# Routing the second mixture of experts inside the attention ahead of it, in pieces, with result adds, next blocks and zone loads ordered behind named instructions

## The chip, the core and the metric

The kernel runs on one core of a Trainium2 chip. A core has five engines, each with an instruction queue that it works off in order: TensorE (PE, matmuls and transposes; its weight loads are listed as PEld), VectorE (DVE), ScalarE (ACT), GpSimd (POOL) and SyncE (SP), which here only reads registers and issues DMAs. ACT and POOL issue some DMAs as well. An instruction waits for its operands, and all that stands behind it in its queue waits too. The metric is the device time of one execution in microseconds (us), lower is better; a profile adds what each engine did when.

## The reference, cut to what matters

A residual stream of 16 sequences of 256 tokens, 4096 tokens of 128 numbers in float32, passes six layers, each with a layer norm ahead of it:

```
x = x + 0.5 * moe(ln(x))      # 8 experts, the best 2 of each token, plus a gated shared expert
x = x + gqa(ln(x))            # softmax attention: 16 query heads on 4 key heads, 8 numbers a head
x = x + 0.5 * moe(ln(x))      # the same weights again
x = x + 0.5 * zones(ln(x))    # the best 3 of 8 feed-forwards, chosen once for a whole sequence
x = x + mla(ln(x))            # attention with latent keys and values, 8 heads
x = x + 0.5 * zones(ln(x))
```
```
def moe(x):
    scores = softmax(x @ gate_w.T)                 # 8 experts
    w = scores * in_top2(scores)
    g, u = split(x @ experts_gate_up)              # 2 x 176, of each expert
    out = sum_e(w[e] * ((silu(g) * u) @ experts_down[e]))
    shared = (silu(x @ sg.T) * (x @ su.T)) @ sd.T  # 352 wide
    return out + sigmoid(x @ shared_gate.T) * shared
```

The change touches the way into and out of both mixtures of experts (MoE), and what is interleaved with the first attention. It computes the same.

## The kernel before

**Tiling.** The stream stays on chip in eight tiles `xs[t]`, one for each block of 512 tokens (two sequences). Two blocks are a pair (four pairs, `q`), two pairs are a part (two parts). The layers follow one another, so the stages in time are: first MoE, attention (`gqa`), second MoE, zones, `mla`, zones.

**The MoE.** A pair is routed in four steps. `norm_pair` normalises its eight 128-token groups (`normalised`, L272: per group `bn_stats` and `bn_aggr`, then one reciprocal square root of some ten small DVE instructions, then eight applies, alternately on DVE and ACT). `turn_pair` transposes the rows on PE (L401). `choose` multiplies them with the router (L417) and finds the best two experts in some 20 small DVE instructions (L425 to L446). `place_pair` counts with three matmuls (L467 to L473) where each token's row goes in a buffer in memory that has a region for each expert, and POOL writes the normalised rows there with 16 indirect DMAs (L486), which read the buffer `xn8`, of which there are two. When a part's two pairs are placed, `moe_tables` closes every region with a block of zeros (eight DMAs on SP, L520) and works out a table: which expert and which row each of 23 tiles of 256 rows takes. `expert_tiles` then runs the 46 tiles as a pipeline three steps deep: step k fetches tile k (SP: the expert's weights, L626, and 256 rows, L631; six buffers each) and transposes it, runs the first product of tile k-1 (`up`, L651 to L660), and the second of tile k-2 (`down`, L673 to L687; ACT issues the write of the result, L687). A dictionary `hooks` names functions that are called after step k. `shared_expert(t)` is dense work for one block. `first_results` asks for the results of blocks 0 to 3 (POOL, eight indirect reads a block, L708), and puts the adds of all eight blocks into `pending`; `add_results` adds a block's eight results to its stream on DVE (L724) and asks for block t+4's. Whoever normalises a block first (`normalised`) runs its pending adds ahead of that.

**The attention.** `gqa` goes over 16 sequences, n = 0 to 15, and four more steps to empty its pipeline. Each n has eight places k = 0 to 7. At each, `units` issues a piece of the scores of sequence n (`score`, L854), the reduction of their largest values on DVE (L891), the scores of sequence n-2 once more in the other layout (`again`, L866) and their exponentials on ACT (L895). Between them come the transposition of the largest values (`send_largest`, with row DMAs on SP), the weighing of the values (`weigh`), the division (`over_sums`) and the output projection (`project`). At every even n the next block is normalised (`gqa_pre`), which pops that block's pending adds; its projections go piece by piece into the places that follow, and POOL adds the output bias to its stream (L813). The routing of pairs 0, 1 and 2 of the second MoE and its first table are handed over by `moe_ahead` as a list, which `gqa` begins to use at n = 16.

**Order.** The program doesn't fix the order on an engine wholly: the build arranges each engine's instructions by due time, so that work written later can come earlier in the queue where its operands allow, ahead of work written before it.

**The zones.** `zones_pre` normalises a block, chooses three of eight zones for each of its two sequences, and loads their six matrices of 512 KB on SP (L1056 reads the number from the result, L1058 loads). `moe_second` calls it for block 0 at step 35 of its tiles, `mla` at its step 16.

## Time and profile before

| | us |
|---|---|
| runs of the kernel | 1622.77, 1632.44, 1621.12 |
| median | 1622.77 |
| the profiled execution | 1630.41 |
| its span, first to last instruction | 1628.6 |

The mean granted clock of PE over that execution is 0.934 of full speed. Its engines and DMA queues as a whole:

```profile
PE 1484.8 (91%) x9010; PEld 971.2 (60%) x9010; DVE 962.7 (59%) x3132; ACT 573.1 (35%) x968; POOL 274.3 (17%) x330
```
```profile
L486 POOL DMA_INDIRECT moe_rows<-xn,moe_slot x128 | 123.5, 965 | 246.8 <-DVE moe_w L504 178.6
L708 POOL DMA_INDIRECT y<-moe_y,moe_index x128 | 122.2, 955 | 235.6 <-DVE moe_shT L597 70.2
```
```profile
zone_m<-in_w_z_dram SPq DMA_DIRECT2D x96, 512.0 KB
moe_we<-in_w_ex_dram SPq DMA_DIRECT2D x92, 312.0 KB
moe_xg<-moe_rows SPq DMA_DIRECT2D x92, 128.0 KB
```

In the first line, busy us, share of the span and number of instructions stand for each engine. In the next two, POOL's indirect writes and reads: line, engine, operation, output and inputs, count; busy us in all and mean ns of one; the idle time before them and what ended most of it. The last three are DMAs that SP issues, with their count and size.

The stages in time, with the busy us of PE and DVE, the number of POOL's busy us, and the clock that was granted to PE, rounded:

| stage | from, to (us) | PE | DVE | POOL | clock |
|---|---|---|---|---|---|
| first MoE: routing | 0, 60 | 42.9 | 39.1 | 31.6 | 0.89 |
| first MoE: tiles | 118, 240 | 111.4 | 78.2 | 33.0 | 0.96 |
| first MoE: last results | 240, 282 | 31.0 | 24.6 | 31.5 | 0.84 |
| attention: first two sequences | 282, 330 | 45.9 | 32.0 | 1.3 | 0.61 |
| second MoE: tiles, up to the hole | 686, 839 | 138.2 | 96.9 | 58.2 | 0.94 |
| second MoE: shared experts | 856, 929 | 65.5 | 42.0 | 30.1 | 0.92 |
| zones | 929, 1118 | 187.1 | 92.0 | 6.8 | 0.99 |
| `mla` | 1118, 1435 | 299.4 | 199.5 | 6.3 | 0.97 |
| zones | 1435, 1628 | 187.4 | 81.6 | 0.0 | 1.00 |

A busy us at a low clock does less work than one at full clock, so both columns have to be read together.

### The profile page before, as it was taken

The page shows a single profiled execution, that of the slowest core. Times are in us where ns is not written, and L with a number is a line of the kernel's source. Part 1 is how long each engine was busy: PE and PEld are TensorE (multiplying, and loading weights), DVE is VectorE, ACT ScalarE, POOL GpSimd, SP SyncE. Part 2 cuts the span into 40 slices and gives each one's busy share as a digit, 9 for nine tenths or more (in the row PEclk, how much of TensorE's full clock was granted, in tenths as well). Part 3 has the DMA queues.
Part 4 walks back from the last instruction along what each step waited for, and adds up shares of the span by engine and source line. Part 5 has one row for each costly group of instructions (what it writes and reads, how often), then busy time and mean ns, then how long its engine had stood idle before and what let it go on. Part 6 is the DMA issues. An engine that isn't in the chain of part 4 may idle for free.

```text
span 1628.6 us, 26384 instructions
## 1 busy us (share of the span) xinstructions
PE 1484.8 (91%) x9010; PEld 971.2 (60%) x9010; DVE 962.7 (59%) x3132; ACT 573.1 (35%) x968; POOL 274.3 (17%) x330
## 2 busy tenths in 40 slices
PE   7779897999999999499859899998999999999998
PEld 4568664445454544276547588885444444468887
DVE  7545676677777763474664745535666666654432
ACT  3324331055555554143233234332323222234432
POOL 4740626000000001741601600001000000000000
PEclk9789898599999997699879899999999999899999
DMA  4447751000000000476354143330000000124342
GB/s 130 132 147 216 214 145 49 1 2 2 2 2 2 2 2 12 126 221 180 100 178 137 46 156 134 118 137 2 2 2 2 2 2 2 64 77 152 134 157 91
DMA packets 107541, 133.61 MB, mean 82 GB/s; under 512 B 13328, under 2 KB 78864, under 8 KB 107408
## 3 DMA queue, kind: packets, MB, share of 16 engines
q1 hardware_dynamic: 74192, 103.07, 20.6%
q0 software_dynamic: 8192, 16.79, 3.4%
q10 hardware_dynamic: 25024, 12.06, 2.5%
q8 instruction: 72, 1.18, 0.3%
q14 instruction: 61, 0.50, 0.1%
HBM read 104.62 MB, written 26.74 MB: 81 GB/s over the span
## 4 chain that ended last, share of the span: by engine, by line
PE 74%; DVE 7%; POOL 6%; issue 5%; DMA 4%; SPq 3%; ACT 1%; DVEq 0%; ACTq 0%; POOLq 0%
PE pa L1073 11%; PE pb L1087 10%; PE score L854 7%; PE pa L651 6%; PE exp L866 5%; PE score L1206 4%; POOL y L708 4%; PE pb L1272 4%; PE pb L917 3%; PE exp L1245 3%; PE exp L1255 2%; POOL moe_rows L486 2%; PE pb L827 2%; PE pa L673 2%; PE pa L678 2%
## 5 line engine op out<-in xcount | busy, mean ns | idle before, releaser
L891 DVE TENSOR_REDUCE nm<-score 128x2 f32<-128x512 f32 x256 | 165.0, 684 | 72.0 <-PE exp L866 57.8
L1073 PE MATMUL pa<-xnT,zone_m 128*128 128x256 f32 x768 | 188.0, 385 | 1.0 <-DVE x L611 1.0
L895 ACT ACTIVATE pT<-exp 128x512 f32<-128x512 f32 x256 | 140.5, 595 | 129.1 <-PE exp L866 128.2
L854 PE MATMUL score<-kT,qT 32*128 32x256 f32 x1024 | 176.1, 430 | 7.7 <-DVE nm L891 7.5
L1087 PE MATMUL pb<-zh,zone_m 128*128 128x256 f32 x768 | 179.8, 381 | 0.0
L866 PE MATMUL exp<-qT,kT 32*128 32x512 f32 x512 | 176.7, 664 | 0.0
L854 PEld LDWEIGHTS score<-kT,qT 32*128 32x128 f32 x1024 | 108.8, 198 | 109.3 <-DVE nm L891 59.1
L1081 ACT ACTIVATE zh<-pa 128x1024 f32<-128x1024 f32 x96 | 98.1, 1023 | 194.4 <-PE pa L1073 194.2
L486 POOL DMA_INDIRECT moe_rows<-xn,moe_slot x128 | 123.5, 965 | 246.8 <-DVE moe_w L504 178.6
L708 POOL DMA_INDIRECT y<-moe_y,moe_index x128 | 122.2, 955 | 235.6 <-DVE moe_shT L597 70.2
L1087 PEld LDWEIGHTS pb<-zh,zone_m 128*128 128x128 f32 x768 | 144.8, 190 | 19.4
L1073 PEld LDWEIGHTS pa<-xnT,zone_m 128*128 128x128 f32 x768 | 143.9, 192 | 19.8 <-DVE x L611 1.1
L651 PE MATMUL pa<-moe_xT,moe_we 128*128 128x256 f32 x552 | 147.6, 404 | 1.7 <-DVE moe_xT L641 1.0
L1213 DVE TENSOR_REDUCE nm<-score 128x4 f32<-128x1024 f32 x64 | 77.1, 1204 | 64.7 <-PE score L1206 64.6
L1259 ACT ACTIVATE pT<-exp 128x1024 f32<-128x1024 f32 x64 | 62.2, 1021 | 148.9 <-PE exp L1255 148.9
L651 PEld LDWEIGHTS pa<-moe_xT,moe_we 128*128 128x128 f32 x552 | 100.8, 198 | 16.7 <-DVE moe_xT L641 2.2
L588 PE MATMUL pa<-moe_xnT,w_sg 128*128 128x512 f32 (+1 forms) x192 | 97.2, 643 | 3.5 <-DVE x L611 2.5
L653 ACT ACTIVATE moe_sg<-pa 128x256 f32<-128x256 f32 x92 | 35.3, 383 | 166.6 <-PE pa L651 158.1
L1206 PE MATMUL score<-kt,qa 64*128 64x256 f32 x512 | 76.7, 409 | 11.6 <-DVE qa L1188 10.2
L1280 DVE RECIPROCAL rs<-pb 128x256 f32<-128x256 f32 x32 | 56.2, 1756 | 39.5 <-PE pb L1272 39.5
L1206 PEld LDWEIGHTS score<-kt,qa 64*128 64x128 f32 x512 | 44.8, 188 | 58.2 <-issue 23.5
L602 PE MATMUL pa<-w_sd,moe_shT 128*128 128x128 f32 (+1 forms) x384 | 57.1, 299 | 22.3 <-DVE moe_shT L597 19.9
(246 smaller groups left out, 2216.0 us busy)
## 6 DMA issues: line engine op xcount, KB each, us to landing
zone_m<-in_w_z_dram SPq DMA_DIRECT2D x96, 512.0 KB
moe_we<-in_w_ex_dram SPq DMA_DIRECT2D x92, 312.0 KB
moe_xg<-moe_rows SPq DMA_DIRECT2D x92, 128.0 KB
moe_y<-moe_yt ACTq DMA_DIRECT2D x92, 128.0 KB
moe_rows<-zero_rows SPq DMA_DIRECT2D x32, 128.0 KB
x<-in_x_dram SPq DMA_DIRECT2D x8, 256.0 KB
moe_rows<-xn,moe_slot POOLq DMA_INDIRECT x128
y<-moe_y,moe_index POOLq DMA_INDIRECT x128
```

The lines of the kernel that those rows point to most:

```text
L486: nc.gpsimd.indirect_dma_start(out=part["views"].pop()[:, :], out_offset=bass.IndirectOffsetOnAxis(ap=slot[:, k, i : i + 1], axis=0), in_= ...
L588: nc.tensor.matmul(ps[0:m, u, :], w_sg[:, u * SI0 + c * P : u * SI0 + c * P + m], xnT, start=True, stop=True,)
L651: nc.tensor.matmul(dst, q["w"][:, cols], q["xT"], start=True, stop=True)
L708: nc.gpsimd.indirect_dma_start(out=y[:, k, i, :], out_offset=None, in_=part["y"][:, :], in_offset=bass.IndirectOffsetOnAxis(ap=part["index ...
L854: nc.tensor.matmul(sc[:, j % 2, :], qa[rows, j, ts(b * NST + st, P)], kt[rows, ts(b, SEQ)], start=True, stop=True,)
L866: nc.tensor.matmul(sc, kt[rows, ts(b * NST + s, P)], qa[rows, ts(half, 2), ts(b, SEQ)], start=True, stop=True,)
L891: nc.vector.tensor_reduce(new["nm"][:, s, g1 + c, ts(half, 2)], scores[c], AX.X, ALU.max, negate=True)
L895: nc.scalar.activation(old["pT", half][:, s, g0 + c, :], exps[c], AF.Exp)
L1073: nc.tensor.matmul(ps[:, f, :], mats[b * K1 + k][:, 0, ts(f, P)], xnT[:, ts(b, SEQ)], start=True, stop=True,)
L1081: nc.scalar.activation(h, ps, AF.Gelu_apprx_tanh)
L1087: nc.tensor.matmul(pz, mats[b * K1 + k][:, 1, ts(f, P)], h[:, f, :], start=(f == 0), stop=(f == NF1 - 1),)
L1206: nc.tensor.matmul(sc[:, p, slot, :], qa[rows, 2 * half + slot, ts(b * NST + st, P)], kt[rows, ts(b, SEQ)], start=True, stop=True,)
```

## The change

1. **Pieces.** `norm_pair` and `turn_pair` are replaced by `pair_pieces`, nine functions: four of statistics, one with the square root, two of applies, two of transposes. `normalised` is left for single blocks, and only it pops pending adds. The operations of one pair are the same.
2. **Row buffers.** The first MoE takes its normalised rows from the stage's pool with four buffers; the second keeps two.
3. **First MoE.** The weights of `mla` are combined (`weights()`) after the shared expert of block 1 instead of block 4; four shared experts instead of five stand ahead of the tiles, four behind; table 1 is worked out after tile step 2 instead of ahead of the tiles; the attention's first block is prepared at step NSLOT + 9 instead of NSLOT + 14.
4. **Hooks.** A hook is now called under `tc.issue_after` of the last DVE product of `up`: its instructions on DVE are put behind that product. `expert_tiles` gives back the last tile's row fetch.
5. **Attention.** `moe_ahead` gives a dictionary from (n, k) to a piece. Pair 0 begins at n = 8, pair 1 at n = 12, each over some three and a half sequences, table 0 stands at (16, 2), pair 2 from n = 16 on. Each piece is called under `tc.issue_after` of the last score reduction (L891), and so is `gqa_pre(t + 1)` for n > 0, with the pending adds that it pops.
6. **Second MoE.** Pair 3 is routed in pieces at steps 0, 2 and 4, chosen at 6, placed at 9 (was 10), table 1 at 11 (was 13); `zones_pre(0)` at NSLOT + 9 (was NSLOT + 12).
7. **Zone loads.** `zones_pre` gives back a function that loads. For block 0 of the first zones it is called after the last results are asked for, behind the last tile's row fetch; for block 0 of the last zones after `mla`'s program; for other blocks at once, as before.

```diff
-    def norm_pair(S, q):
-        S["xn"][q] = normalised(2 * q, 2)
-
-    def turn_pair(S, q):
-        for c in range(2):
+    def pair_pieces(S, q):
+
+        src = [xs[2 * q + i // NTT][:, i % NTT, :] for i in range(NPT)]
+        p = {}
+
+        def stats(c):
...
+            for i in range(2 * c, 2 * c + 2):
+                nc.vector.bn_stats(p["st"][:, i, :], src[i])
+                nc.vector.bn_aggr(p["mv"][:, i, :], p["st"][:, i, :])
+
+        def root():
+            p["y"] = rsqrt(p["mv"][:, :, 1], NPT)
...
+            S["xn"][q] = S["pool"]().tile([P, NPT, D], F32, name="pair_xn", bufs=S["rows"])
...
+        return (
+            [partial(stats, c) for c in range(4)]
+            + [root]
+            + [partial(apply, c) for c in range(2)]
+            + [partial(turn, c) for c in range(2)]
+        )
```
```diff
+        pool, rows = ((lambda: stage["pool"]), 4) if m == 0 else ((lambda: routed), 2)
```
```diff
             for f in hooks.get(k, ()):
-                f()
+                if "up" in last:
+                    with tc.issue_after(last["up"].ins):
+                        f()
+                else:
+                    f()
+        return last["fetch"]
```
```diff
         shared_expert(S, 1)
+        weights()
         route(S, 3)
-        moe_tables(S, 1)
-        for t in range(2, 5):
+        for t in range(2, 4):
             shared_expert(S, t)
-        weights()
         hooks = {
+            2: [partial(moe_tables, S, 1)],
             NSLOT + 1: [partial(first_results, S)],
-            NSLOT + 14: [lambda: result.append(after())],
+            NSLOT + 9: [lambda: result.append(after())],
         }
...
-        for t in range(5, NBLK):
+        for t in range(4, NBLK):
             shared_expert(S, t)
```
```diff
     def moe_ahead(S):
...
+        at = {}
+        for q, first in ((0, 8), (1, 12)):
+            places = (0, 2, 4, 6, 8, 10, 12, 16, 18, 22, 28)
+            pieces = pair_pieces(S, q) + [partial(choose, S, q), partial(place_pair, S, q)]
+            for k, f in zip(places, pieces):
+                at[first + k // 8, k % 8] = f
+        at[16, 2] = partial(moe_tables, S, 0)
+        pieces = pair_pieces(S, 2) + [partial(choose, S, 2), partial(place_pair, S, 2)]
+        for k, f in zip((3, 4, 5, 6, 7, 8, 9, 11, 12, 15, 19), pieces):
+            at[16 + k // 8, k % 8] = f
+        return at
```
```diff
-                    rest = gqa_pre(t + 1) if t + 1 < NBLK else None
+                    rest = None
+                    if t + 1 < NBLK:
+                        with tc.issue_after(reduced["last"].ins) if n else ExitStack():
+                            rest = gqa_pre(t + 1)
...
-                if n >= 2 * NBLK and k % 2 == 1 and tail:
-                    tail.pop(0)()
-        for f in tail:
-            f()
+                if (n, k) in ahead:
+                    with tc.issue_after(reduced["last"].ins):
+                        ahead[n, k]()
```
```diff
-            0: [partial(norm_pair, S, 3)],
-            4: [partial(turn_pair, S, 3)],
+            0: third[0:4],
+            2: third[4:7],
+            4: third[7:9],
             6: [partial(choose, S, 3)],
-            10: [partial(place_pair, S, 3)],
-            13: [partial(moe_tables, S, 1)],
+            9: [partial(place_pair, S, 3)],
+            11: [partial(moe_tables, S, 1)],
             NSLOT - 1: shared[0:2],
             NSLOT + 1: [partial(first_results, S)] + shared[2:4],
-            NSLOT + 12: [lambda: result.append(after())],
+            NSLOT + 9: [lambda: result.append(after())],
         }
-        expert_tiles(S, hooks)
+        fetched = expert_tiles(S, hooks)
         last_results(S)
+        with tc.issue_after(fetched.ins):
+            ready = result[0]()
```
```diff
-        mats = []
-        for b in range(NB):
-            for k in range(K1):
...
-        return xnT, w, mats
+        def load_zones():
+            mats = []
+            for b in range(NB):
+                for k in range(K1):
...
+            return xnT, w, mats
+
+        return load_zones
...
-                    ready = zones_pre(t + 1)
+                    ready = zones_pre(t + 1)()
...
-        ready = mla(ready, partial(zones_pre, 0))
+        ready = mla(ready, partial(zones_pre, 0))()
```

## The prediction

> **What bounds the kernel now.** I read the engines' shares first: TensorE (PE) is busy 91% of the span, so what can be won is the time in which it waits or runs at a reduced clock. Then the stretches between the stages:
>
> ```profile
> 9.00:94.00 85.00, 71.37 (x363) 49.65 (x364) 56.36 (x316) 27.56 (x50) 51.63 (x54) 0.88 0.42 118
> ...
> 235.00:282.00 47.00, 35.91 (x130) 20.70 (x129) 26.07 (x96) 7.36 (x13) 31.52 (x33) 0.85 0.18 51
> ```
> ```profile
> 330.00:603.00 273.00, 266.96 (x2091) 137.68 (x2090) 209.88 (x467) 149.05 (x277) 5.04 (x4) 0.99 0.01 2
> 603.00:686.00 83.00, 60.12 (x294) 28.56 (x292) 31.75 (x157) 24.05 (x51) 33.68 (x35) 0.72 0.15 47
> ...
> 839.00:856.00 17.00, 1.24 (x7) 0.72 (x6) 3.44 (x22) 1.66 (x2) 0.00 (x0) 0.50 0.70 247
> ```
>
> Columns: length, busy time of PE, PE weight loads, VectorE (DVE), ScalarE (ACT), GpSimd (POOL), granted PE clock, DMA share, GB/s. The steady attention (330 to 603) is full: PE 267 of 273 us, DVE 210. The holes lie around it: the end of the first MoE, the attention's tail, 17 empty us in the second MoE. Their causes, from the timelines (start, duration, in brackets the idle time before and what ended it). End of the attention's tail, in the chain of waits:
>
> ```profile
> 681.29 2.23 DMA moe_rows<-xn,moe_slot
> 684.02 2.12 DMA moe_xg<-moe_rows
> 686.27 0.67 PE pb L639 x2
> ```
> All 32 scatters of pairs 0 and 1 run one by one on POOL from 641.96 to 682.25, and the first expert rows are read after the last of them. The hole at 839, in SyncE's DMA queue and on PE:
>
> ```profile
> 842.77 6.28 SPq L1058 DMA_DIRECT2D zone_m<-in_w_z_dram  x6
> 849.29 0.33 SPq L626 DMA_DIRECT2D moe_we<-in_w_ex_dram  x1
> ```
> ```profile
> 856.03 0.66 PE L639 MATMUL pb<-ident,moe_xg 128*128 128x128 f32 x2 [15.79 <-DMA moe_xg<-moe_rows]
> ```
> The zone loads sit in the queue ahead of ten expert tiles, waiting for block 0's zone routing. And the result adds, hoisted early into DVE's in-order queue, wait for gathers with the experts' work behind them:
>
> ```profile
> 174.97 0.61 DVE L724 SCALAR_TENSOR_TENSOR x<-y,moe_w,x 128x128 f32<-128x128 f32 x2 [2.86 <-DMA y<-moe_y,moe_index]
> ```
> ```profile
> 177.51 1.19 PE L673 MATMUL pa<-moe_we,moe_h 128*128 128x128 f32 x4 [4.11 <-DVE h L660]
> ```
>
> **The change part by part.** All against the profiled run, 1630.4 us (span 1628.6); the median shown is 1622.8, so 7.6 us come off at the end.
>
> (a) First MoE, rows in four buffers. With two, pair 2's normalised rows wait for pair 0's scatters: PE waits 5.97 us (to 48.9) and 2.09 us (to 69.2), and in 50 to 60 it is busy 9.42 us at a clock of 0.52, 4.5 us lost: 12.6 us. Part 0's scatters end at 68, its rows are read at 69, the first tile runs at 94.4; so the gain is not stopped by POOL, though DVE at 9.97 of 10 us in 30 to 40 takes some of it. I take -9. Shared expert 4 only changes place (8 us off here, 8 back in c). MLA weights earlier: half of the 3.0 us wait at 87 to 90, -1. Table 1 behind tile 2: its eight zero-row writes hold SyncE 9.1 us; now they starve tile 6 by 4.4 us (to 111.8), later they fall among the first fetches, 2.3 us each against 2.53 us a tile. Between +5 and -7, I take -3. Sum -13 (-4 to -20).
>
> (b) Adds of block 0 behind tile 31's up. Its gathers start at 168.3, 1.25 us each, so the eighth lands about 180.5; 26 tiles are up at 168.3, tile 31 is at about 181. The 4.11 us wait and about 1 us of clock go. Block 1's adds get no pin (there is no score reduce yet at n = 0), so the second wait (3.34 us, to 191.4) stays. -5 (-2 to -10).
>
> (c) Adds of blocks 2 to 7 behind score reduces. In 235 to 282 DVE waits 12.9 us on gathers in 17 pieces. PE's work there at full clock is three shared experts at 8.2 us and the first block's projections, some 30 of 47 us. -15 (-8 to -18). The last gathers, 40 us of POOL, now run under the attention, which has POOL busy 5 us in 273.
>
> (d) Attention fuller. Two pairs' transposes (2.2 us), router matmuls (1.95) and placing (1.4) are 5.5 us of PE each, +11. On DVE, choose is a burst of some 20 instructions at 0.25 us, 5 us. What a burst costs is shown here: rsqrt and its neighbours before one reduce stretch the reduce pitch from 2.1 to 5.0 us,
>
> ```profile
> 430.94 1.29 DVE L891 TENSOR_REDUCE nm<-score 128x2 f32<-128x512 f32 x2 [0.85 <-PE exp L866]
> ...
> 435.89 1.28 DVE L891 TENSOR_REDUCE nm<-score 128x2 f32<-128x512 f32 x2
> ```
> and PE loses 1.08 us in 435 to 440. So three score banks cover about 2.6 us of a 3.7 us burst: two chooses cost 5, stats, root and place in pieces up to 2.4 us about 1. Pinned next blocks: adds 2.4, stats 1.9, rsqrt 2.4, apply 1.1, 7.8 us of DVE; in one piece 5.2 us each, six times 31, less some 8 paid already: +23; cut up by reduces, 0. No row shows which; the bursts of before were cut in places, so I take +10. Sum +27 (+14 to +42). ACT (149 of 273 us) covers the rows' applies; without that cover they cost 8 x 0.48. POOL's 40 us of scatters delay only the bias adds L813, due four steps later; SyncE's table writes at (16, 2) stand after the last row sends.
>
> Here a rule speaks against the change. POOL beside a busy DVE:
>
> ```profile
> 30.79 0.96 POOL L486 DMA_INDIRECT moe_rows<-xn,moe_slot  x1 [0.30 <-issue]
> ```
> In that stretch DVE is 99% busy and the scatter takes 0.96 us as it does elsewhere. The Trainium skill (SBUF — State Buffer, section SBUF: two separate sides) says that GpSimd can't write the descriptors of its DMAs while VectorE holds their shared port; its section A bandwidth-pool intuition that's wrong gives 620 ns growing to 3100. By that, an estimate, a scatter's pitch goes from 1.26 to 3.7 us, pair 1's take 59 instead of 20 us, and since they start about 10 us before n = 16, table 0's rows are ready some 49 us into the tail: nothing or 5 us lost. I go by the row: nothing.
>
> (e) Tail, n = 16 to the first tile. Now 83 us. Left: 16 score-again steps at 1.06 us, 12 weighings at 1.06, turns and projections 8, pair 2's 5.5: 43 us at full clock. Scatters of part 0 are long done and pair 2's rows no longer wait for pair 0's (8.4 us at 663.8). The clock is the open term: PE is busy 10 of 10 us in 630 to 640 at 0.65. The Trainium skill (TensorE: Matmul & The Clock Gate, section What's actually happening) has the clock restored by some 3.4 us of busy PE; so the tail would be 43 us. By the row, half of it stays slow: 60 us. I take 46, as the router's small matmuls of two pairs, where the clock fell, leave. -37 (-22 to -45).
>
> (f) Second MoE, block 0's adds behind tile 31: PE waits of 1.48 and 1.93 us go, block 1's 0.81 and 3.76 stay (unpinned). -4 (0 to -10).
>
> (g) Zone loads behind the last fetch: 15.8 us of wait, and half clock to 860. -18 (-12 to -20). The loads take 6.3 us of issue; zones start 55 us after the last fetch (872 to 927), which covers them; uncovered they would cost some 15 us. The same form before the last zones moves loads that issue at 1416 for use at 1435: 0 (to +5).
>
> (h) Pair 3 in pieces and table 1 two tiles sooner, blocks after 884: 0 (-4 to +4).
>
> Sum: -13 -5 -15 +27 -37 -4 -18 = -65. 1630.4 - 65 = 1565; on the median 1558.
>
> **The rivals.** R1: the attention takes most of it back. Bursts in one piece (d at +42) and a slow tail (e at -22): -35, 1588. For it: DVE goes from 210 to nearly 240 of 273 us. Against: reduces did cut into bursts.
>
> R2: pins don't hold what they name. Block 1's adds, unpinned, stand first in DVE's queue and wait there for the whole gather: b, c and f give nothing: -41, 1582. For it: adds of block 1 floated to 182 and 794 before. Against: blocks 4 to 7 are what fills 242 to 272.
>
> R3, slower: after PE's waits in the attention the clock stays down, as in 290 to 330 (busy 39 of 40 us, clock 0.55). Price: half a us for each us of steady attention at half clock. From 130 us on (mean clock 0.76) the gain of 65 is gone; at 200 us, 1658. Against: after the 1.08 us gap at 435 the clock stayed 1.00; after that at 340 it was 0.66 for only 5 us.
>
> **How the numbers follow.** The sum: 0.60 (own range 1535 to 1580); R1 0.19; R2 0.12; R3 with its milder forms 0.09. Predicted 1558. The range 1518 to 1600 takes in R1 and R2, and a and e at their better ends. 1% is 16 us, about what a measurement of this kernel can tell: faster 0.87, within 0.06 (R1 with a poor a), slower 0.07.
>
> **What would show it.** The scatters of pairs 0 and 1 under the attention at 0.96 us; the first tile 42 to 50 us after the last score reduce; no zone_m issue before the last moe_we; no L724 wait at the first MoE's end; steady attention about 300 us. Wrong if that grows beyond 320, if PE waits for moe_xg remain, or if its clock in the attention falls below 0.95.

## The result, and the profile after

| | us |
|---|---|
| kernel after, median of 20 runs | 1623.83 (1618.5 to 1628.09) |
| kernel before, median of 20 runs beside it | 1633.03 (1621.12 to 1639.99) |
| ratio, with its 95% interval | 0.995 [0.9932, 0.9968] |
| profiled execution after | 1622.86, span 1621.1 |

The change gains half a per cent where about four were forecast. In two groups of runs below (e1 to e4, e8 to e11) every kernel takes longer, the kernel before 1804 and 1810 us, as PE, DVE and ACT stand idle together for up to 15 us at a time, for a reason that no run here shows, so these runs are read against others of their own group, and against the rest only to a few us.

The stretches that the prediction showed of before, now of the kernel after (the same columns: length, busy time of PE, weight loads, DVE, ACT, POOL, granted clock, DMA share, GB/s):

```profile
9.00:94.00 85.00, 72.30 (x418) 51.95 (x418) 61.95 (x331) 31.29 (x61) 51.48 (x54) 0.98 0.43 120
235.00:282.00 47.00, 45.71 (x211) 27.50 (x210) 22.02 (x42) 9.21 (x15) 15.11 (x16) 0.96 0.10 26
330.00:603.00 273.00, 263.54 (x1953) 136.01 (x1952) 214.34 (x572) 136.18 (x256) 30.76 (x31) 0.93 0.03 8
603.00:686.00 83.00, 78.53 (x394) 33.59 (x393) 38.81 (x160) 34.22 (x66) 18.63 (x20) 0.76 0.17 49
839.00:856.00 17.00, 12.81 (x55) 9.56 (x53) 13.62 (x85) 5.68 (x11) 0.00 (x0) 0.63 0.14 35
```

Every hole that the change aimed at is filled: PE is busy 45.71 of 47 us at the end of the first MoE (35.91 before), 78.53 of 83 in the tail, 12.81 of 17 at 839. Yet the time hardly moves. To see why, the span is cut at events that both kernels have. "Idle" is time without a running PE instruction, "lost" is PE's busy time multiplied by one minus the granted clock, both worked out from the two traces:

| stretch | before: us, idle, lost | after: us, idle, lost |
|---|---|---|
| start to first expert tile | 94.4, 22.6, 8.5 | 71.5, 16.8, 1.7 |
| to first score product | 187.9, 26.4, 12.3 | 199.5, 36.2, 4.7 |
| attention, first to last score | 318.4, 8.1, 22.2 | 351.8, 13.0, 45.1 |
| tail, to the second MoE's first tile | 85.6, 23.2, 14.5 | 62.2, 3.8, 16.8 |
| second MoE, to first zone product | 240.5, 37.8, 11.5 | 241.3, 37.5, 12.1 |
| zones, `mla`, zones | 701.7, 25.7, 11.4 | 694.6, 25.9, 3.5 |

(After, the first stretch has one shared expert less, some 8 us, and the second one more.) Both kernels reach the first zone product at the same moment, 926.8 and 926.4 us. What was won in the tail went to the attention; in the two MoEs old holes went and new ones came. The 7 us of the last row are PE's clock in `mla`, which the change doesn't touch: it was at half for 17.1 us before and for none after. Two kernels below with the same `mla`, e16 and e15, differ there in the same way, so it isn't put down to the change.

The new holes, in the timeline of PE of the kernel after (start, duration, in brackets the idle time before and what ended it):

```profile
112.22 0.69 PE L674 MATMUL pb<-ident,moe_xg 128*128 128x128 f32 x2 [19.57 <-DMA moe_xg<-moe_rows]
...
182.06 1.19 PE L708 MATMUL pa<-moe_we,moe_h 128*128 128x128 f32 x4 [9.62 <-DVE h L695]
...
790.62 3.40 PE L621 MATMUL pa<-moe_xnT,w_sg 128*96 128x512 f32 x4 [4.44 <-DVE x L644]
...
800.14 0.80 PE L635 MATMUL pa<-w_sd,moe_shT 128*128 128x128 f32 x2 [4.14 <-DVE moe_shT L630]
```

**Tile 6 waits 19.57 us for its rows.** The queue of SyncE in the kernel after:

```profile
81.34 0.38 SPq L666 DMA_DIRECT2D moe_xg<-moe_rows  x1
98.97 0.36 SPq L661 DMA_DIRECT2D moe_we<-in_w_ex_dram  x1
100.19 8.87 SPq L553 DMA_DIRECT2D moe_rows<-zero_rows  x8
109.25 0.39 SPq L666 DMA_DIRECT2D moe_xg<-moe_rows  x1
```

Nothing is issued from 81.7 to 98.97, and no wait is named. The lines of the register loads, in the listing of L659 and L662 for 80 to 100 us, fill it (count, duration in ns as least, median and most, first and last start):

```profile
L659 SPq TENSOR_LOAD <-moe_table x14: 261/316/558, 81.8 to 98.1; - x14
```
```profile
L662 SPq TENSOR_LOAD <-moe_table x14: 263/268/484, 80.5 to 97.5; - x14
```

These are the table entries of fourteen tiles to come, pulled ahead of the fetch of one; each brings two small register instructions along, so that 27 of them take 17.2 us, 0.64 each. The Trainium skill (DMA: Bandwidth & Descriptors, section Latency and other measured facts) gives about 600 ns as the least for such a load. In this trace that fits the distance from one load to the next (0.56 us at the least), while the record of a load alone is 0.26 to 0.56 us. Then come the eight zero writes of table 1, each with a register load of its own.

The same queue in the kernel before:

```profile
81.19 0.38 SPq L631 DMA_DIRECT2D moe_xg<-moe_rows  x1
90.37 9.14 SPq L520 DMA_DIRECT2D moe_rows<-zero_rows  x8
...
109.11 0.40 SPq L631 DMA_DIRECT2D moe_xg<-moe_rows  x1
```

There too 27 such loads and the eight zero writes stand between the rows of tile 5 and those of tile 6, which are asked for at 109.11, against 109.25 now. Moving table 1 has only changed the order in between. The hole was 4.39 us before because PE began its tiles at 94.4; now it begins at 71.5 and waits for the same moment.

**Tile 25's second product waits 9.62 us, and shared experts wait at 790 and 800.** DVE, kernel after:

```profile
169.28 0.42 DVE L676 COPY moe_xT<-pb 128x256 f32<-128x256 f32 x1
179.31 0.35 DVE L764 SCALAR_TENSOR_TENSOR x<-y,moe_w,x 128x128 f32<-128x128 f32 x1 [9.60 <-DMA y<-moe_y,moe_index]
180.63 0.35 DVE L764 SCALAR_TENSOR_TENSOR x<-y,moe_w,x 128x128 f32<-128x128 f32 x1 [0.97 <-DMA y<-moe_y,moe_index]
180.90 0.41 DVE L692 TENSOR_TENSOR moe_h<-moe_sg,pa 128x256 f32<-128x256 f32 x1
```

The adds at 179.31 are not block 0's, which is pinned, but block 1's, which has no pin and now stands first; its gathers (POOL issues them from 176.66 on) come behind block 0's eight (from 166.61 on). In the second MoE the free blocks 1, 2 and 3 do the same from 780 to 812.

**The attention's bursts.** DVE around 361 us, kernel after:

```profile
358.59 1.29 DVE L945 TENSOR_REDUCE nm<-score 128x2 f32<-128x512 f32 x2 [0.74 <-PE exp L918]
...
360.34 0.68 DVE L894 TENSOR_TENSOR v<-pb,b_v 128x512 f32<-128x512 f32 x1
360.93 1.66 DVE L764 SCALAR_TENSOR_TENSOR x<-y,moe_w,x 128x128 f32<-128x128 f32 x6
...
363.76 0.66 DVE L945 TENSOR_REDUCE nm<-score 128x2 f32<-128x512 f32 x1
```
```profile
364.48 0.48 PE L906 MATMUL score<-kT,qT 32*128 32x256 f32 x1 [1.90 <-DVE nm L945]
```

A pinned block's adds and statistics stand between two reductions in one piece, the reductions come 5.2 us apart, and PE waits 1.90 us for a score bank. Waits of this kind, 1.31 to 1.90 us, end at 364, 406, 449, 493 and 543, and with all but the first comes a stretch of 3.4 to 6.8 us at half clock. The whole of the attention, first to last score, before and after:

```profile
282.30:600.70 318.40, 310.29 (x2254) 162.06 (x2253) 239.59 (x534) 151.89 (x279) 6.31 (x5) 0.93 0.01 2
271.00:622.90 351.90, 338.86 (x2314) 176.06 (x2314) 264.44 (x687) 154.07 (x285) 41.15 (x41) 0.87 0.03 8
```

Of the 22.9 us more that the clock takes here, 21.6 fall after the first two steps, where the pinned bursts stand.

**The tail's clock.** PE is busy all the time in these 20 us, at a granted clock of 0.50:

```profile
640.00:650.00 10.00, 10.00 (x30) 3.27 (x29) 1.10 (x4) 3.94 (x8) 0.00 (x0) 0.50 0.01 2
650.00:660.00 10.00, 10.00 (x35) 3.01 (x32) 1.77 (x6) 2.17 (x4) 0.00 (x0) 0.50 0.00 1
```

### The profile page after: what moved, and what is told of

Same layout as the page of the kernel before. It is cut to its first block, busy times and chain, and to the rows that moved or that the text cites. A ratio compares the mean times of both kernels' runs of the same rounds, so it can differ in the third digit from the quotient of the medians.

```text
span 1621.1 us, 26387 instructions
## 1 busy us (share of the span) xinstructions
PE 1487.8 (92%) x9010; PEld 966.1 (60%) x9010; DVE 957.4 (59%) x3132; ACT 573.3 (35%) x968; POOL 274.2 (17%) x330
## 4 chain that ended last, share of the span: by engine, by line
PE 76%; DVE 10%; POOL 4%; issue 4%; SPq 3%; DMA 2%; ACT 1%; DVEq 0%; POOLq 0%; ACTq 0%
PE pa L1134 11%; PE pb L1148 10%; PE score L906 7%; PE pa L686 5%; PE exp L918 5%; PE pb L971 4%; PE score L1267 4%; PE pb L1333 4%; POOL y L748 4%; PE exp L1306 3%; PE pa L621 3%; PE exp L1316 2%; PE pb L879 2%; PE pa L708 2%; PE pa L635 2%
## 5 line engine op out<-in xcount | busy, mean ns | idle before, releaser
L906 PE MATMUL score<-kT,qT 32*128 32x256 f32 x1024 | 188.6, 458 | 12.9 <-DVE nm L945 12.7
L918 PE MATMUL exp<-qT,kT 32*128 32x512 f32 x512 | 190.5, 717 | 1.4 <-ACT pT L949 1.4
L906 PEld LDWEIGHTS score<-kT,qT 32*128 32x128 f32 x1024 | 113.3, 210 | 121.1 <-DVE nm L945 60.4
L519 POOL DMA_INDIRECT moe_rows<-pair_xn,moe_slot x128 | 123.6, 966 | 205.7 <-DVE moe_w L537 98.2
L1267 PE MATMUL score<-kt,qa 64*128 64x256 f32 x512 | 75.7, 405 | 11.8 <-DVE qa L1249 10.2
L692 DVE TENSOR_TENSOR moe_h<-moe_sg,pa 128x256 f32<-128x256 f32 x92 | 38.6, 419 | 77.0 <-ACT moe_sg L689 76.5
L708 PE MATMUL pa<-moe_we,moe_h 128*128 128x128 f32 x368 | 59.7, 286 | 22.9 <-DVE h L695 21.6
```

What stands on the lines that cost most here:

```text
L519: nc.gpsimd.indirect_dma_start(out=part["views"].pop()[:, :], out_offset=bass.IndirectOffsetOnAxis(ap=slot[:, k, i : i + 1], axis=0), in_= ...
L906: nc.tensor.matmul(sc[:, j % 2, :], qa[rows, j, ts(b * NST + st, P)], kt[rows, ts(b, SEQ)], start=True, stop=True,)
L918: nc.tensor.matmul(sc, kt[rows, ts(b * NST + s, P)], qa[rows, ts(half, 2), ts(b, SEQ)], start=True, stop=True,)
L1267: nc.tensor.matmul(sc[:, p, slot, :], qa[rows, 2 * half + slot, ts(b * NST + st, P)], kt[rows, ts(b, SEQ)], start=True, stop=True,)
```

## The experiments

The theory: three in-order queues (SyncE's loads, DVE's free blocks in either MoE) took back the gain in the MoEs, and the pinned next blocks, not the pair pieces, took it back in the attention, by waits and by the clock. (Work is pinned where `tc.issue_after` puts it behind a named instruction, and free where the build places it by due time.) The rivals: holes that only move when one is filled, and pieces as the cause. All kernels start from the kernel after.

| run | what | median | before beside it | ratio [95%] |
|---|---|---|---|---|
| r_changed_again | kernel after | 1623.14 | 1629.63 | 0.9961 [0.9947, 0.9976] |
| e5 | pin zone blocks 1 to 3 | 1594.08 | 1629.63 | 0.9804 [0.9772, 0.9836] |
| e6 | e5, block 1's pin, loads in turn | 1572.54 | 1629.63 | 0.9674 [0.9638, 0.971] |
| e7 | e6, adds in first steps, norms free | 1559.37 | 1629.63 | 0.9576 [0.9543, 0.961] |
| e12 | loads in turn alone | 1617.1 | 1631.42 | 0.9913 [0.9892, 0.9933] |
| e13 | block 1's pin alone | 1611.72 | 1631.42 | 0.9884 [0.9814, 0.9954] |
| e14 | e7 with zone loads at once | 1576.11 | 1631.42 | 0.9666 [0.96, 0.9732] |
| e15 | e7 with shared experts in steps 0, 1 | 1546.05 | 1631.42 | 0.9486 [0.9435, 0.9537] |
| e16 | e15, loads in turn in first MoE only | 1544.06 | 1632.14 | 0.9455 [0.943, 0.9479] |
| e1, e2 | as e13, as e12 | 1795.99, 1794.87 | 1804.16 | 0.9945, 0.9944 |
| e3, e4 | pairs in the tail; next blocks free | 1814.74, 1784.59 | 1804.16 | 1.0056, 0.9867 |
| e8, e9 | as e13, as e12 | 1802.08, 1801.45 | 1809.66 | 0.9956, 0.9954 |
| e10, e11 | as e14, as e15 | 1820.26, 1790.41 | 1809.66 | 1.0073, 0.9887 |

The medians are of two runs in e13 and e14, of four or five in e5, e6, e7, e15 and e16, and of fifteen in e12. The yardstick, on the chip that also ran e5, e6 and e7:

> The changed kernel itself, as the yardstick on the chip that runs the next three. The first four experiments ran on a chip where the kernel before took 1804 us instead of 1633 and all engines stood still several times for 10 to 14 us while POOL wrote rows; there the ratios of single experiments could not be laid against the changed kernel's. Here: a ratio of 0.992 to 0.998 to the kernel before, whatever chip it is; if below 0.990 or above 1.000, the change's worth depends on the chip.

It holds: 0.9961, and each stretch is within 5 us of the first profile of the kernel after.

### Free blocks in the second MoE (e5)

```diff
-                    ready = zones_pre(t + 1)()
+                    with tc.issue_after(up_of["last"]) if s == 3 and t < 3 else ExitStack():
+                        ready = zones_pre(t + 1)()
```

(`up_of["last"]` is the last DVE product of the MoE's tiles.)

> The changed kernel with blocks 1 to 3 of the first zones (result adds, norm, choice) put behind the last DVE product of the second MoE's 46 tiles; the change left them free, and in the changed kernel's profile their adds stand in DVE's queue from 780 to 812, waiting for 24 gathers at 1.25 us, while PE waits 4.4, 1.5 and 4.1 us. Theory: these waits go and 2 to 3 us of half clock with them; the second MoE's tiles take 180 to 186 us instead of 193, total 7 to 12 us below the changed kernel beside it. Rival (three blocks' adds and norms behind the tiles now crowd the shared experts, 48 us): that stretch grows by as much and the total moves by less than 4 us.

The second MoE, from first tile to first zone product, in e5:

```profile
682.10:891.20 209.10, 193.65 (x1072) 143.73 (x1070) 136.53 (x503) 75.91 (x178) 81.72 (x86) 0.97 0.58 169
```

209.1 us against 241.6 in the yardstick: 24.3 less in the tiles and 8.2 less in the shared experts, which the rival had growing. The direction is the theory's, the size (29.1 us in the medians) three times what I had expected. I had added up PE's waits of 1.5 us and more. In this stretch PE's idle time falls from 37.5 to 15.5 us in all, and the time lost to the clock from 12.6 to 4.9.

### Register loads and block 1 (e1, e2, e6, e8, e9, e12, e13)

```diff
-                        with tc.issue_after(reduced["last"].ins) if n else ExitStack():
+                        with tc.issue_after(reduced["last"].ins if n else up_of["last"]):
```
```diff
-            e = nc.sync.value_load(table[0:1, 0, k : k + 1], min_val=0, max_val=E0 - 1)
+            with tc.issue_after(last["fetch"].ins) if "fetch" in last else ExitStack():
+                e = nc.sync.value_load(table[0:1, 0, k : k + 1], min_val=0, max_val=E0 - 1)
+                r = nc.sync.value_load(
+                    table[0:1, 1, k : k + 1], min_val=0, max_val=E0 * REGION - SLOTS
+                )
...
-            r = nc.sync.value_load(
-                table[0:1, 1, k : k + 1], min_val=0, max_val=E0 * REGION - SLOTS
-            )
```

The first is block 1's pin, the second the loads in turn. Alone each was run three times.

> The changed kernel (1623.8 us) with one pin more: the attention's second block (its result adds, statistics and norm) is put behind the last DVE product of the first MoE's 46 tiles, where the change left it free. Theory: the wait of 9.6 us on PE at 169.7 (tile 25's second product, behind block 1's adds in DVE's queue) goes, with 1 to 2 us of half clock after it, and nothing takes its place: 1611 to 1615, attention starting at about 260 instead of 271. Rival (the same adds only wait elsewhere, ahead of the shared experts or of the first score reductions): 1620 to 1626, with a new wait of over 5 us between 227 and 300.

> The changed kernel with the register loads of each tile's table entry kept behind the fetch of the tile before it, so that SyncE does two loads ahead of each fetch instead of 27 in a row (17.2 us from 81.7 to 99.0). Zero writes of table 1 stay where they are. Theory: the 19.6 us hole on PE from 92.6 to 112.2 is made of these 27 loads and the eight zero writes (8.9 us); without the loads in a row tile 6's rows are asked for at about 91 instead of 109, the hole shrinks to 2 to 5 us, and the time falls by 13 to 18: 1606 to 1611. Rival 1 (the zero writes or POOL's indirect writes, which end at 107.8, hold the fetch): hole stays above 14 us, 1619 to 1625. Rival 2 (loads are then late for later tiles): several waits of 1 us or more on tile rows after tile 8.

> The pin of block 1 alone once more (the first time the chip's own standstills covered it). Theory: the 9.6 us wait at tile 25 goes, ratio to the kernel before 0.988 to 0.991 where the changed kernel has 0.996: 8 to 12 us. Rival (only together with the loads is it worth anything, as the holes overlap): 0.994 to 0.997.

> The register loads in turn alone once more. Theory: the 19.6 us hole shrinks to 2 to 5 us, ratio 0.985 to 0.989. Since the run with three pins is 21.5 us under the run with the zone pin alone, this and the run before should share about 21 us between them, 13 to 16 of it here. Rival: the hole is the zero writes' and POOL's, ratio above 0.993.

Taken alone, ratios of 0.9944 to 0.9956 would speak for the rivals, but their intervals overlap, and PE has waits of 12 to 21 us among the tiles in each of them (e1: 19.8, for nothing that the trace names) that the kernel after doesn't have, so these four decide nothing. Together, beside the yardstick:

> Three pins together on the changed kernel: block 1 of the attention behind the first MoE's last tile product, blocks 1 to 3 of the zones behind the second MoE's, and each tile's register loads behind the fetch before it. Theory (holes in in-order queues are what took back the change's gain ahead of and behind the attention): 9.6 + about 14 + about 9 us less than the changed kernel beside it, 25 to 35 us, attention starting 20 to 26 us earlier. Rival (these holes are only the form that a shortage of DMA or POOL time takes, so that filling one opens another): less than 12 us.

From first tile to first score e6 takes 170.7 us (yardstick 197.8), and the attention starts 26.5 us earlier. In all 50.6 us less: more than expected, because of e5's share. Then apart:

> Register loads in turn, alone. On a chip where the kernel before takes about 1630 us: the first MoE's stretch from first tile to first score falls from 198 to 180 to 185 us with no wait on tile rows over 4 us, total 13 to 17 us under the changed kernel's 1623. Rival (block 1's wait takes it back): that stretch stays above 192 us. On a chip of about 1805 us: nothing to be read, as before.

> Block 1's pin alone. On a chip of about 1630 us: the same stretch 187 to 190 us, the wait at tile 25 gone, total 8 to 11 us under 1623; together with the run before 21 to 26 us. Rival: under 4 us.

Waits of PE from first tile to last in e13 and in e12 (us in total, times, longest):

```profile
PE pb L676 <- DMA moe_xg<-moe_rows: 21.7, 4, 19.5
...
PE pa L710 <- DVE h L697: 1.9, 2, 1.6
```
```profile
PE pa L709 <- DVE h L696: 11.3, 5, 8.4
PE pb L675 <- DMA moe_xg<-moe_rows: 6.2, 5, 3.5
```

Each takes its own hole away and leaves the other: 8.4 stays in e12, 19.5 in e13. In e12 tile 6's rows are asked for at 95.78, behind the same eight zero writes (85.89 to 95.6), and PE waits 3.50 us, while POOL writes rows until 108.96. So most of the hole was the loads; the zero writes leave 3.50 us, and POOL's writes did not hold the fetch. Block 1's pin is worth 11.4 us in the medians (e13 has two runs) and 11.3 in this stretch (186.5 us). The loads in turn win 13 us in it (185.2 us), but e12 ends only 6 us under the yardstick, not 13 to 17: its second MoE takes 199.3 us for the tiles instead of 193.5. Whether loads in turn do that was asked last:

> As the run with shared experts in the first two steps (1546 us), with register loads kept in turn in the first mixture alone. Theory (in the second mixture the loads in turn leave SyncE too little lead over the tiles): its tiles take 166 to 171 us instead of 175.6, total 1537 to 1542. Rival (the difference between those runs comes from the later or earlier start of the stage, not from the loads): 174 to 178 us and 1544 to 1548. On a chip of about 1805 us nothing can be read.

Tiles of the second MoE: 172.3 us against 175.6 in e15, totals 1544.06 and 1546.05. That lies between theory and rival and inside the intervals. e6 against e5 points the same way (177.5 and 169.2 us for these tiles), so loads in turn seem to cost some 3 to 8 us in the second MoE; why is not shown.

### Pieces or pinned blocks (e3, e4, e7)

```diff
-        for q, first in ((0, 8), (1, 12)):
...
+        for q in range(3):
+            pieces = pair_pieces(S, q) + [partial(choose, S, q), partial(place_pair, S, q)]
+            if q == 2:
+                pieces = [partial(moe_tables, S, 0)] + pieces
+            for k, f in enumerate(pieces):
+                k += (0, 0, 11)[q]
+                at.setdefault((16 + k // 8, k % 8), []).append(f)
...
```

> The changed kernel with the pieces of pairs 0 and 1, table 0 and pair 2 all placed from n = 16 on; the steady attention has only its own work and the pinned next blocks. Theory: the pieces are what stretches steps 8 to 14 (157.9 us against 135.7 before), so these come back to 135 to 142 us; the last score reduction ends near 604 instead of 624; the tail grows from 62 to 80 to 95 us; in all 1620 to 1640. Rival (the pinned next blocks stretch these steps too): steps 8 to 14 stay above 148 us, and the total is over 1640.

```diff
-                        with tc.issue_after(reduced["last"].ins) if n else ExitStack():
+                        with ExitStack():
```

> The changed kernel with the next blocks (result adds, statistics, norm) of the attention not pinned behind a score reduction. Theory: the pinned bursts of 7.8 us stretch steps 2 to 7 (127.7 us against 118.1 before) and part of 8 to 14; free, steps 2 to 7 take 117 to 122 us, and the adds of blocks 2 to 7 go back to the end of the first MoE, where DVE waits for gathers: that stretch (227.7 to the first score) grows from 43 to 52 to 58 us. In all 1618 to 1630. Rival (pins cost nothing, the pair pieces do): steps 2 to 7 stay at 125 to 130 us and the total goes to 1634 or more.

```diff
+        with tc.issue_after(up_of["last"]):
+            for t in (2, 3):
+                pending.pop(t)()
+        for t in range(4, NBLK):
+            ahead[(t - 4) // 2, 4 * (t % 2) + 3] = pending.pop(t)
...
-                        with tc.issue_after(reduced["last"].ins if n else up_of["last"]):
+                        with ExitStack() if n else tc.issue_after(up_of["last"]):
```

> As the run with three pins, and the attention's next blocks no longer pinned in the full steps: adds of blocks 2 and 3 stand behind the first MoE's last tile product, those of blocks 4 to 7 behind score reductions of n = 0 and 1, where DVE is busy about 5 of 10 us; norms are free. Theory (DVE bursts in full steps cost PE its banks and then its clock): steps 2 to 9 take 18 to 20 us each as before the change, the stretch from first score to last 320 to 332 us instead of 352, and the total is 40 to 55 us below the changed kernel beside it. Rival (the bursts cost the same wherever they stand, or the first two sequences are DVE's bound): steps 0 and 1 grow from 47 to over 58 us, and the total stays within 10 us of the run with three pins.

In e7 the adds of blocks 2 and 3 stand behind the first MoE's last tile product, those of blocks 4 to 7 behind reductions of steps 0 and 1, and the norms are free. A step runs from its first score reduction to the next step's. In us:

| | steps 0, 1 | 2 to 7 | 8 to 14 |
|---|---|---|---|
| before | 44.3 | 118.1 | 135.7 |
| after | 47.0 | 127.7 | 157.9 |
| e3: pinned blocks, no pieces | 46.1 | 136.7 (e1, e2: 134.6, 134.9) | 143.9 |
| e4: pieces, free blocks | 44.3 | 114.7 | not read (step 11 is 34.4 us long) |
| e7: pieces, adds in steps 0 and 1 | 45.4 | 119.8 | 144.7 |

Both theories have a part. Without the pieces, steps 8 to 14 keep 8.2 of the 22.2 us that they grew by; without the pinned blocks, steps 2 to 7 are back at 115 to 120, and steps 8 to 14 keep 9.0. So pieces and pinned blocks share the later steps, the 5 us that are left coming only with both, and the earlier steps are the pinned blocks' alone. In e7 the stretch from first to last score is

```profile
246.30:575.50 329.20, 320.91 (x2314) 169.85 (x2313) 253.26 (x627) 153.89 (x285) 32.19 (x32) 0.92 0.02 7
```

329.2 us where the kernel after takes 351.8: the pins cost 22.6 us, the pieces the 10.8 that remain over the kernel before. Against e6, from which e7 differs in these blocks alone, it is 16.7 us (345.9) and 13.2 in the medians. Nearly all of the 22.6 is the clock: it takes 24.4 us in e7 and 45.1 in the kernel after, idle time 8.3 and 13.0. The total was expected 40 to 55 us under the yardstick and is 63.8 under it. Free blocks gain even if their adds go back to the end of the first MoE: e4 pays 22 to 25 us there (76.0 us against 51.5 and 54.1 in e1 and e2), wins 30 to 34 in the attention, and its ratio is 0.9867 where e1 and e2 beside it have 0.9945 and 0.9944. And the pieces seem worth their price: e3's tail takes 119.7 us against 75.7 in e1, with a ratio of 1.0056; but 37.5 us of e3's tail are idle time, which need not all be the pieces'.

### The zone loads (e10, e14)

```diff
-            NSLOT + 9: [lambda: result.append(after())],
+            NSLOT + 9: [lambda: result.append(after()())],
...
-        with tc.issue_after(fetched.ins):
-            ready = result[0]()
+        ready = result[0]
```

> The fastest version so far (1559 us) with the change's seventh point undone: block 0's zone loads are asked for as soon as its zones are chosen, ahead of the last tiles' fetches in SyncE's queue. Theory (the point is worth what the prediction said, and was only hidden by other waits): a hole of 10 to 16 us on PE about tile 36 to 38, second MoE's tiles 179 going to 189 to 197 us, total 1569 to 1577. Rival (the zones' choice now comes so late or so early that the loads stand in nobody's way): 1557 to 1562.

> Zone loads at once, on the version with all pins. In the last call the second MoE's tiles took 245.8 us with this and 231.0 without, on a chip with standstills. Here on a chip of about 1630 us: 189 to 197 us against 177 to 180, total 1569 to 1577 where the same version with late loads took 1559. Rival: below 183 us.

In e14 the second MoE's tiles take 195.7 us where e7 has 179.2, and the hole of before is back, in SyncE's waits and on PE:

```profile
SPq L1127 <- DVE zone_w L1115: 25.0, 1, 25.0
```
```profile
801.76 0.66 PE L677 MATMUL pb<-ident,moe_xg 128*128 128x128 f32 x2 [17.44 <-DMA moe_xg<-moe_rows]
```

1576 (two runs) against 1559 us: the point is worth 16.7 us, and 16.5 in the second MoE alone (235.6 and 219.1 us). e10 against e11, which also moves two shared experts, has 245.8 and 231.0 us for the tiles.

### The clock of the first two steps (e11, e15)

Shared experts 6 and 7 leave the stretch ahead of the attention:

```diff
...
+        for e in range(2):
+            for k, f in enumerate(shared_pieces(moes[0], NBLK - 2 + e)):
+                filler[e, 2 * k + 1] = f
...
+                if (n, k) in filler:
+                    with tc.issue_after(reduced["last"].ins), tc.issue_after(reduced["score"].ins):
+                        filler[n, k]()
```

> The fastest version so far with the shared experts of blocks 6 and 7 (8.2 us of PE each at full clock) taken out of the stretch ahead of the attention and cut into four pieces each between the units of n = 0 and n = 1, in the exp banks, which are free there; each piece is put behind the last score product and the last reduction. Theory (in n = 0 and 1 PE has too little to do, and its clock falls to half for that): the stretch ahead of the attention goes from 43 to about 27 us, steps 0 and 1 stay at 21 to 25 us because the clock stays up (under 10 us of half clock in them, 34 before), total 1540 to 1546. Rival (the half clock there has another cause, such as products of only 32 rows, and the pieces just add their time at half clock): steps 0 and 1 take 32 us or more each, total 1557 to 1575.

> Shared experts of blocks 6 and 7 in the attention's first two steps, with all pins and late zone loads. In the last call these two steps had 3.4 us at half clock of 51 us. Here on a chip of about 1630 us: 1540 to 1546. Rival (the stretch ahead of the attention needs that work to cover POOL's last reads, which end about 30 us after the last tile): 1552 to 1560, with waits for gathered results on DVE ahead of the first reduction.

Steps 0 and 1 in e7, and in e15:

```profile
248.80:294.20 45.40, 42.79 (x162) 24.36 (x160) 34.71 (x90) 4.43 (x6) 6.99 (x7) 0.62 0.03 7
```
```profile
234.90:289.20 54.30, 47.13 (x234) 25.17 (x232) 48.70 (x150) 8.60 (x13) 18.93 (x19) 0.94 0.09 22
```

16 us of PE work more in the two steps cost 8.9 us, since the clock goes from 0.62 to 0.94; the stretch ahead falls from 43.3 to 27.7. The steps take 26.5 and 27.8 us, more than the 21 to 25 expected of e11, but half clock is down from 34.1 to 6.8 us (3.4 in e11). The total, 1546.05, is at the upper end of what was expected, 13 us under e7. So other products put between the scores bring the clock back; that the pieces merely add their time at half clock is ruled out. Whether it is their amount or their shape (128 rows, where a score product has 32) is not told apart by this run. (The later steps hold the same score products among others, and from 370 to 400 in the kernel after the clock was 1.00.) The Trainium skill (TensorE: Matmul & The Clock Gate, section A second HAM failure mode: psum-queue depth-cycling) tells of short idle times between groups of products that make the clock go up and down. The two lines don't show this as the cause: PE idles 2.6 of 45.4 us in e7, and more, 7.2 of 54.3 us, in e15, where the clock is up. e15 and e16 are 5.1% and 5.5% under the kernel before, and beat both kernels.

## Why the prediction was wrong, step by step

The forecast was -65 us on the profiled run; it moved by 7.5, of which 7.1 are the clock of `mla`, which nobody forecast. By stretch, in us against the kernel before, with the shared expert of 8 us counted where it stood before:

| stretch | forecast | kernel after | e7 |
|---|---|---|---|
| start to first tile (a) | -10 | -14.9 | -13.0 |
| to first score (a's table 1, b, c) | -23 | +3.6 | -23.0 |
| attention (d) | +27 | +33.4 | +10.8 |
| tail (e) | -37 | -23.4 | -22.8 |
| second MoE (f, g) | -22 | +0.8 | -21.4 |

The step that failed is the pricing of the queues in the two MoEs: the sum took off what each moved piece had cost, and put at nothing what then stands in front of the work that is left, SyncE's register loads ahead of tile 6 (a) and the free blocks' adds on DVE (b, f). The two rows miss by 26.6 and 22.8 us. Two terms were mis-sized besides, both by PE's clock: the pinned next blocks (d, 6.4 us) and the tail (e, 13.6 us). With the queues put right, e7's MoEs come out nearly as forecast; its attention and its tail miss by 16 and 14 us in opposite directions, so that its 1559 us are the 1558 forecast for the change is in part luck.

- **(a)** The row buffers did what was forecast: the waits of 5.97 and 2.09 us are gone. What failed is table 1 behind tile 2, put at -3 "between +5 and -7". It priced the eight zero writes. In front of them stood 27 register loads, 17.2 us, which neither busy times nor waits show, and the hole grew from 4.39 to 19.57 us. In the kernel before the same loads stood on both sides of the zero writes, thirteen ahead and fourteen in the 9 us without an issue from 99.5 on; the prediction put the whole wait down to the zero writes.
- **(b)** Block 0's pin holds. The prediction said that block 1 stays free and charged its old wait of 3.34 us; with block 0 out of the way it moved forward and cost 9.6. That is rival R2's mechanism in one place: 11.4 us (e13).
- **(c)** Right. The wait for 17 gathers is gone; the stretch from the last tile's transpose to the first score fell from 52.0 to 43.3 us with one shared expert (some 8 us) more in it, about 17 us against 15.
- **(d)** +27 forecast, +33.4 measured. The pieces were put at 17 and cost 10.8. The pinned next blocks were put at 10, between 0 and 23, because bursts of before had been cut by reductions; they cost 22.6 (16.7 against e6), the end that a burst in one piece gives. That end was worked out from waits, though, and most of the cost is the clock, which the sum had at nothing: time lost to it in this stretch rose from 22.2 to 45.1 us, idle time from 8.1 to 13.0. That is R3's mechanism at a quarter of R3's 93 us (1658 against 1565); R1 had the right place. The sign that the prediction named came, a clock under 0.95 (0.93 from 330 to 603), as did PE's wait for `moe_xg`.
- **(e)** -37 forecast, -23.4 measured, the end of the range. The work was right (43 us at full clock forecast, 41.6 measured), the clock wrong: 34 us at half clock cost 16.8. I had gone nearer to the Trainium skill's rule (TensorE: Matmul & The Clock Gate, section What's actually happening) that some 3.4 us of busy PE restore the clock than to the row that showed 10 of 10 busy at 0.65. Here PE is busy 20 of 20 us at 0.50. The row decides; by it the tail was put at 60 (half of 43 us at half clock makes rather 64), and it took 62.2.
- **(f), (g)** -22 forecast, +0.8 measured. The zone loads' -18 is right in size (16.7 in e14 against e7), but the free blocks 1 to 3 and what stands behind them cost more than that: 32.5 us in e5, whose second MoE is 31.4 us under the kernel before. The prediction looked at waits of 0.81 and 3.76 us of block 1 alone and never asked what the other free blocks would do.
- The port rule that was weighed and set aside: POOL's writes under the attention take 0.96 us each, 1.26 us apart, as the row said, not 3.1.

In one sentence: the prediction asked of each pinned piece where it goes, and not of each piece left free what comes forward into the room.

## What to carry to other kernels

When work is pinned behind an instruction in a queue that a scheduler fills, list what is left unpinned: it moves up, and if it waits for a transfer, everything behind it waits too. Count the register loads on a DMA-issuing queue as work of 0.64 us each, since no busy time shows them, and ask of a wait that goes away whether the next queue was early enough to profit. Work that has to be tucked into a full stage belongs where the engine that feeds TensorE has slack: here adds in the first two steps, and shared experts between their scores, were worth 13 us each. Whether next blocks cut into shorter pieces would have done in the full steps was not run.

## What the runs showed of the hardware

- PE stayed at half clock for 24 us while the trace has it busy without a gap (636.5 to 660.4 in the kernel after, 23.90 of 23.90 us). A busy PE is thus no sign of a full clock. Nor does the share of weight loads tell: they were busy 3 of 10 us here, but 24.36 of 45.40 us in e7's first two steps, at 0.62. What decides it is not settled by these runs.
- `mla`, unchanged, took 318.0 us in e15, 318.0 in the kernel after, 325.2 in e16 and 325.3 in the kernel before (from the last zone product ahead of it to the first behind it). The longer two had 17.1 us at half clock, the others none. A single profile carries that much chance, nearly as much as the whole change won.
